# Choosing side tasks by deadline instead of by arrival in a TensorE-bound attention kernel

## The chip, the cores and the metric

The kernel runs on one core of a Trainium2 chip. The core has several engines that work side by side, each through its own list of instructions in order: TensorE (PE, matrix products), VectorE (DVE), ScalarE (ACT, exponentials and copies), GpSimd (POOL, here mostly a second issuer of transfers) and SyncE (SP, which issues most transfers). An engine waits for another by semaphores. The metric is the device time of one execution in microseconds (us): 3230.17 us is the median of three runs of the kernel before (3229.19 to 3231.65).

## The reference

The input `x` is 4 images of 256 channels, 64 x 64 pixels, in float32. Two residual layers follow each other. Both normalize their input in groups of eight channels (`_gn`) and attend with 8 heads of 32 channels.

```python
# layer 0: keys and values come from 2x2 blocks of pixels (1024 keys)
q = jnp.einsum('oc,bchw->bohw', Wq, x)
k = lax.conv_general_dilated(x, Wk, window_strides=(SR, SR), ...)
v = lax.conv_general_dilated(x, Wv, window_strides=(SR, SR), ...)
attn = einsum(q, k) + einsum(q, rel_h + rel_w)
out = einsum(v, softmax(attn * scale))
# layer 1: attention inside four areas of 1024 pixels, a depthwise 7x7 convolution of v, a projection
out = einsum(softmax(q k * scale), v) + _dwconv7(v_full, w_pe, b_pe)
return _conv1x1(out, w_proj, b_proj)
# around them
x = x + layer0(_gn(x)); x = x + layer1(_gn(x))
```

## The kernel before, in words

**Units, steps and phases.** The work is cut into 8 blocks: layer 0 of the four images ("A", b), then layer 1 of the four ("B", b). A block has 16 units; a unit is 512 queries of four heads against 1024 keys. A unit has 8 key steps of 128 keys. The main loop runs in 683 phases, and a phase covers one and a half steps: `scores` (L311) makes the scores of one whole and one half step, ScalarE takes their exponentials (L349, L360), VectorE adds them up for the denominators (L384), and in the next phase `weighted` (L374) multiplies them with the values. A step s falls into phase 2s/3, rounded down. A unit takes 5.33 phases.

**Side work.** Everything else must find room in the phases: normalized inputs, q, k and v, the depthwise convolution, the output projection. `plan_a` and `plan_b` (and `plan_values`, `plan_conv`) write down by `at(unit, step, f)` when a piece is due to be emitted. Loads, normalizations (`normalize`, one ScalarE instruction each, L276), statistics and additions are emitted directly at the end of the phase of their step. Products on TensorE are Python generators put into the list `side` by `task`; each `yield` ends a part. Between the scores and the weighted sums of a phase `side_parts` emits some parts of the first task in the list. All of them share one PSUM bank ("side"), which ScalarE or VectorE empties.

**The order of side work.** `side` is first in, first out. `soon_tasks` puts the q products (L540 and L639) and the projection (L695) at its front. The sum of parts waiting sets the pace: over 4, two parts in a phase; over 8, four; otherwise one. A phase in which a unit's denominators are due (`divisors`, L393) has no other side work. `need` emits side tasks on the spot where the scores ask for a q, k or v that isn't there yet.

**The convolution.** `plan_values` makes the values of an image (`values`, evicted at L833 into one of two `vout` buffers) and stores them to memory in two forms (L838, L846). `load_share` loads, for eight channels, a band matrix (L884) and four sets of rows (L887) from memory. `convolve` (L903) multiplies two such shares, 32 matmuls each, and calls `load_share` for the next ones after each half. There is room for two shares, or three from the second image on. All these transfers are issued by SP in the order of emission, and SP waits where a buffer isn't free.

**The division.** The sum of exponentials of a unit is copied out (L410), spread over partitions by two transfers of GpSimd (L411, L412), inverted on VectorE (`reciprocals`, L418, two units after the unit's start), and broadcast by five transfers (L420, L422) into `rb`. `multiply` (L425) multiplies it on VectorE with the unnormalized output `av_sb`, three units after the unit's start. `av_sb` has two buffers; ScalarE's copy of a unit's output out of PSUM (`evict`, L974) waits for the multiplication of the unit two before.

Of the kernel before, what the change touches and what calls it, by code (L numbers as in the profile page):

```python
# [59 lines left out]
def direct_path(  # L60
# [128 lines left out]
    side, quick = deque(), deque()  # L189
    now, last = [-1], len(BLOCKS) * UNITS * NKT  # L190

    def task(parts, f, *args):
        side.append([parts, f(*args), False])

    def soon_tasks(tasks):

        for n, (parts, f, *args) in enumerate(tasks):
            side.insert((1 if side and side[0][2] else 0) + n, [parts, f(*args), False])

    def advance():  # L200
        side[0][0] -= 1
# [4 lines left out]

    def need(made, key):
        while key not in made:
            advance()
        return made[key]  # L210


    def begun():
        return bool(side) and side[0][2]

    def soon(f):

# [180 lines left out]
    def divide(g, unit):  # L398

        if g == len(units) - 1:  # L400

            rb = pool.tile([P, CH], FP, tag="p", name="rb", bufs=PB)
            V.reciprocal(rb, dens[g])  # L403
            V.tensor_mul(unit[4]()[:, unit[0], :], avs.pop(g), rb)  # L404
            spare.extend((dens.pop(g), rb))
            return
        den_sb = pool.tile([P, CH], FP, tag="cout", name="den_sb", bufs=2)
        few = pool.tile([P, 2, CH // HD], FP, tag="few", name="few", bufs=2)
        rows = dram.tile([4, CH], FP, tag="rows", name=f"rows_{g}", bufs=4)
        S.copy(den_sb, dens.pop(g))  # L410
        G.dma_start(rows, den_sb[0:P:HD, :])  # L411
        G.dma_start(few[:, 0, :], rows.rearrange("h (q n) -> (h q) n", n=CH // HD))  # L412
        made = {}

        def reciprocals():
            rb = made["rb"] = pool.tile([P, CH], FP, tag="rb", name="rb", bufs=1)
            recs = dram.tile([4, CH], FP, tag="recs", name=f"recs_{g}", bufs=4)
            V.reciprocal(few[:, 1, :], few[:, 0, :])  # L418
            V.tensor_reduce(sums[:, :, g], few, AX.X, ALU.add)  # L419
            G.dma_start(recs.rearrange("h (q n) -> (h q) n", n=CH // HD), few[:, 1, :])  # L420
            for h in range(4):
                G.dma_start(rb[HD * h : HD * h + HD, :], recs[h : h + 1, :].to_broadcast([HD, CH]))  # L422

        def multiply():
            V.tensor_mul(unit[4]()[:, unit[0], :], avs.pop(g), made["rb"])  # L425

        at(*((g + 2, 0) if g < len(units) - 2 else (g + 1, 6)), reciprocals)
        at(*((g + 3, 0) if g < len(units) - 3 else (g + 2, 6) if g < len(units) - 2 else (g + 2, 0)), multiply)

    def att_of(key):  # L430
        if key not in atts:
# [4 lines left out]
    def plan_a(b, u, prep):  # L436
# [35 lines left out]
        def make_k(a, qd):  # L472
            if "k" not in taps:
                taps["k"] = k_tile(key)
            k, ps = taps["k"], ps_side(f"k0ps_{b}_{a}_{qd}")[:, :256]
            for n in range(8):
                t, i, w = n // 4, n // 2 % 2, n % 2
                product(
                    ps, lhsT=wk0_sb[:, t, 2 * i + w, qd * P : (qd + 1) * P], rhs=taps[a][:, t, i, w],
                    start=(n == 0), stop=(n == 7),  # L480
                )
                if n % 2 and n < 7:
                    yield
            S.copy(k[:, qd, a * 256 : (a + 1) * 256], ps)
            if a == NAREA - 1:

                rows = k[:, qd, :].rearrange("p (i j) -> p i j", j=32)
                V.tensor_add(rows, rows, relh_sb[:, qd : qd + 1, :].to_broadcast([P, 32, 32]))
                V.tensor_add(rows, rows, relw_sb[:, qd, :].unsqueeze(2).to_broadcast([P, 32, 32]))
                if qd == 1:  # L490
                    ks[key] = k

        def make_v(a, m):
            if "v" not in taps:
                taps["v"] = v_tile(key)
            v, ps = taps["v"], ps_side(f"v0ps_{b}_{a}_{m}")[:, :C]
# [16 lines left out]
        for a in range(NAREA):  # L513
            g = prep + (2 + 3.4 * a if b else 6 + 2.2 * a)
            at(0, int(NKT * (g - 1.6)), lambda a=a: load(a))
            for n in range(8):
                at(0, int(NKT * (g - 1.1)) + n, lambda a=a, n=n: make_taps(a, n))
            for n in range(2):
                at(0, int(NKT * (g + 0.6 * n)), lambda a=a, n=n: task(4, make_k, a, n))
                at(0, int(NKT * (g + 0.6 * n + 1.2)), lambda a=a, n=n: task(4, make_v, a, n))  # L520

        xcs, hqs, made_q = {}, {}, {}

# [4 lines left out]
            normalize(key, hqs[c][:, t, :], hqs[c][:, t, :], t)  # L528

        def make_q(c, qd):  # L530
            if qd == 0:
                made_q[c] = pool.tile([P, 2, CH], FP, tag="q", name=f"q0_{b}_{c}", bufs=2)
            hq, ps = hqs[c], ps_side(f"q0ps_{b}_{c}_{qd}")
# [44 lines left out]
    def plan_b(b, u):  # L578
# [11 lines left out]
        kvs, vcs = {}, {}  # L590

        def make_k(a, qd, half):
            if qd == 0 and half == 0:
                kvs["k"] = k_tile(("B", b, a))
            k, ps = kvs["k"], ps_side(f"k1ps_{b}_{a}_{qd}_{half}")
# [29 lines left out]
                vs["B", b, a] = v  # L625

        def make_q(c, qd):
            if qd == 0:
                kvs["q"] = pool.tile([P, 2, CH], FP, tag="q", name=f"q1_{b}_{c}", bufs=2)
            q, ps = kvs["q"], ps_side(f"q1ps_{b}_{c}_{qd}")  # L630
# [12 lines left out]
        for a in range(NAREA):  # L643
            g = u + 4 * a
            at(g - 6, 3, lambda a=a: load(a))
            for t in range(CT):
                at(g - 5, 2 + 3 * t, lambda a=a, t=t: norm(a, t))
            for n in range(4):
                at(g - 4, 1 + 4 * n, lambda a=a, n=n: task(2, make_k, a, n // 2, n % 2))
            for n in range(4):  # L650
                at(g - 3, 1 + 2 * n, lambda a=a, n=n: load_v(a, n))
                at(g - 2, 1 + 2 * n, lambda a=a, n=n: make_v(a, n))
        for c in range(NCH):
            at(u + 2 * c - 2, 4, lambda c=c: soon_tasks([(2, make_q, c, qd) for qd in range(2)]))

        rest, made_x = {}, {}

# [2 lines left out]
            nc.sync.dma_start(made_x[c], xmid[b][c])  # L660

        def load_rest(c, t):
            if t == 0:
                rest[c] = chunk_tile(f"cv_{b}_{c}")
            cv = rest[c]
# [62 lines left out]
        for c in range(NCH):  # L728
# [75 lines left out]
            for n in range(TX + 6):  # L804
                at(g + 1, 6 * k + n, lambda k=k, n=n: matrices(k, [n]))

    stored = {}

    def plan_values(b, c, start):

# [8 lines left out]

        def values(t):  # L820
            vout = pool.tile([P, RC, TX, XT], FP, tag="vout", name=f"vout_{b}_{c}_{t}", bufs=2)
            V.memset(vout[:, :, :, 0], 0.0)
            V.memset(vout[:, :, :, 1 + WW // TX :], 0.0)
            h = made["h"]
            ps = ps_side(f"vals_ps_{b}_{c}_{t}")
            for tt in range(CT):
# [26 lines left out]
        when = int(start * NKT)  # L853
        at(0, when - 3, load)
        for t in range(CT):
            at(0, when + 5 + t, lambda t=t: norm(t))
# [6 lines left out]
    def load_share(must):  # L863
# [19 lines left out]
        loaded[b, k] = band, xs  # L883
        nc.sync.dma_start(band, mats[k])  # L884
        for a in range(4):
            p = NP // 2 * (a % 2)
# [8 lines left out]
    def convolve(b, n):  # L895
        size = NY * WW // TX
        ps = ps_side(f"conv_ps_{b}_{n}")
        for k in range(2):
            band, xs = loaded.pop((b, 2 * n + k))
            for i in range(2):  # L900
                for half in range(2):
                    for m in range(4):
# [13 lines left out]
            conv[b][16 * n : 16 * n + 16].rearrange("(i c) m y x -> (c m) i (y x)", i=4), out  # L916
        )
        load_share(False)
        yield
# [69 lines left out]

    def side_parts(budget):  # L990

        mine, done = side[0] if side else None, 0
        while done < budget and side and side[0] is mine:
            advance()
            done += 1
# [4 lines left out]

    f = step = 0
    before = []
    while f < PHASES or before or plan or side or quick or to_add or to_divide:
        now[0] = step
        exps = scores(f) if f < PHASES else [lambda: None] * 3
        mine = []
        if f < PHASES:
# [10 lines left out]
        if cut:  # L1018
            evict(before[0][0] // NKT)
        exps[2]()  # L1020
        waiting = sum(n for n, *_ in side)
        if due and not begun():
            g = to_divide.popleft()
            divisors(g, *([last - 1] if g == final else []))
            if g < final:
                divide(g, units[g])
            waiting = 0
        elif cut or waiting > 4 or due or f >= PHASES:
            side_parts(4 if waiting > 8 else 2)
        elif boundary(mine):  # L1030
            side_parts(1 if begun() else 2 if waiting >= 4 else 0)
        else:
# [613 lines left out]
```

## Time and profile before

| | |
|---|---|
| median of three runs | 3230.17 us |
| the profiled execution's own time | 3217.57 us |
| its span, first to last instruction | 3215.8 us |
| TensorE busy | 3088.3 us (96%) |
| VectorE busy | 2525.9 us (79%) |
| ScalarE busy | 2454.4 us (76%) |
| mean granted TensorE clock | 0.985 |

"Busy" is the time in which at least one instruction of the engine ran. The row PE in the page's second part is TensorE's busy share in 40 slices of the span, in tenths; PEclk is the clock that it was granted. In the list of waits a line says which engine and line waited for whom, the total, the number of times and the longest. In a timeline a line has the start, the length, the engine, the line, the operation, what it writes and reads, how many instructions were merged into it, and in brackets the idle time before it and who ended it. PEld are the weight loads of TensorE, which run beside its matmuls.

### The profile page before, as it was taken

How to read it: one execution, taken by the hardware profiler on the slowest of the kernel's cores; microseconds unless marked ns; L12 is line 12 of the kernel's file. 1: busy time of each engine (PE TensorE's matmuls, PEld its weight loads, DVE VectorE, ACT ScalarE, POOL GpSimd, SP SyncE). 2: the span in 40 equal slices, each digit the busy share in tenths (PEclk: the TensorE clock that was granted, in tenths of full speed). 3: DMA queues.
4: the chain of work that ended last, by engine and by line, in shares of the span. 5: the costliest groups of instructions: out<-in, count | busy, mean ns of one | idle time of the engine just before them, and what ended most of it. 6: DMA issues, size and time to landing. Idle time of an engine off the chain costs nothing. (4 is left out here: it accounts for less than half of the span.)

```text
span 3215.8 us, 87826 instructions
## 1 busy us (share of the span) xinstructions
PE 3088.3 (96%) x36218; PEld 1427.4 (44%) x36218; DVE 2525.9 (79%) x2719; ACT 2454.4 (76%) x2988; POOL 486.9 (15%) x923
## 2 busy tenths in 40 slices
PE   7999999999999999998999999999999999999997
PEld 4444444444344554444444444444444444444442
DVE  3687887778776678787677787888878788888887
ACT  3788778887767788887777787787877777787775
POOL 0111121111211111111111111111111111111111
PEclk9999999999999999999999999999999999999999
DMA  5243433555554564567877665655444656633212
GB/s 182 43 105 77 114 90 93 116 119 128 126 136 132 150 166 126 129 151 184 215 192 188 181 164 142 172 154 128 109 97 121 164 159 160 181 102 85 60 43 72
DMA packets 648235, 422.29 MB, mean 131 GB/s; under 512 B 411772, under 2 KB 556636, under 8 KB 647832
## 3 DMA queue, kind: packets, MB, share of 16 engines
q1 hardware_dynamic: 619384, 380.11, 46.8%
q0 software_dynamic: 28448, 36.48, 4.6%
q8 instruction: 293, 4.80, 0.6%
q14 instruction: 110, 0.90, 0.1%
HBM read 318.32 MB, written 98.09 MB: 129 GB/s over the span
## 5 line engine op out<-in xcount | busy, mean ns | idle before, releaser
L384 DVE TENSOR_TENSOR acc<-acc,p 128x1024 f32<-128x1024 f32 x1790 | 2114.9, 1220 | 533.0 <-PE av L374 234.1
L349 ACT ACTIVATE p<-s 128x1024 f32<-128x1024 f32 x1194 | 1160.2, 1027 | 450.7 <-PE s L311 445.4
L360 ACT ACTIVATE p<-s 128x1024 f32<-128x1024 f32 x598 | 620.7, 1038 | 0.4 <-DVE acc L384 0.3
L311 PE MATMUL s<-q,k_A 32*128 32x256 f32 (+1 forms) x5464 | 568.1, 517 | 20.8 <-ACT p L349 10.9
L311 PE MATMUL s<-q,k_B 32*128 32x256 f32 (+1 forms) x5456 | 553.3, 511 | 3.3 <-ACT p L349 3.0
L311 PEld LDWEIGHTS s<-q,k_A 32*128 32x128 f32 x5464 | 342.5, 186 | 309.3 <-ACT p L349 71.2
L311 PEld LDWEIGHTS s<-q,k_B 32*128 32x128 f32 x5456 | 345.4, 184 | 282.8 <-issue 60.8
L374 PE MATMUL av<-p,v_A 128*32 128x256 f32 (+1 forms) x4784 | 457.4, 494 | 0.0
L374 PE MATMUL av<-p,v_B 128*32 128x512 f32 (+1 forms) x4776 | 450.3, 487 | 0.0
L422 POOL DMA_DIRECT2D rb<-recs x508 | 252.0, 501 | 453.6 <-DMA recs<-few 369.2
L374 PEld LDWEIGHTS av<-p,v_B 128*32 128x32 f32 x4776 | 149.5, 110 | 261.6 <-issue 235.9
L420 POOL DMA_DIRECT2D recs<-few x127 | 70.0, 552 | 1229.8 <-DVE sums L419 1193.2
L374 PEld LDWEIGHTS av<-p,v_A 128*32 128x32 f32 x4784 | 150.7, 111 | 236.0 <-issue 198.2
L349 ACT ACTIVATE acc<-s 128x1024 f32<-128x1024 f32 x172 | 167.0, 1024 | 84.8 <-PE s L311 84.7
L903 PE MATMUL conv_ps<-rows,band 88*32 88x128 f32 x3072 | 109.3, 287 | 39.8 <-DMA rows<-vals 39.1
L393 PE MATMUL den<-acc,ones 128*32 128x512 f32 x1024 | 140.2, 607 | 4.8 <-ACT vout L833 3.3
L412 POOL DMA_DIRECT2D few<-rows x127 | 72.3, 569 | 460.9 <-DMA rows<-den_sb 454.7
L411 POOL DMA_DIRECT2D rows<-den_sb x127 | 74.4, 586 | 408.7 <-ACT den_sb L410 402.6
L164 PE MATMUL ops<-cv,wp_sb 128*32 128x512 f32 x1024 | 126.3, 604 | 5.6 <-DVE cv L680 4.4
L164 PE MATMUL q0ps<-hq,wq_sb 128*32 128x512 f32 x1024 | 126.1, 605 | 0.0
L164 PE MATMUL q1ps<-h,wqkv_sb 128*32 128x512 f32 x1024 | 123.3, 598 | 2.2 <-DVE xm L695 2.2
L164 PE MATMUL k0ps<-taps,wkv 128*32 128x256 f32 x2048 | 122.7, 385 | 2.5 <-ACT taps L276 2.5
(99 smaller groups left out, 2200.4 us busy)
## 6 DMA issues: line engine op xcount, KB each, us to landing
rows<-vals SPq DMA_DIRECT2D x384, 195.9 KB
rb<-recs POOLq DMA_DIRECT2D x508, 64.0 KB, 3.1
share<-vals SPq DMA_DIRECT2D x128, 195.9 KB
vala<-vout SPq DMA_DIRECT2D x128, 144.0 KB
vals<-vout SPq DMA_DIRECT2D x128, 144.0 KB
vc<-vala SPq DMA_DIRECT2D x64, 288.0 KB
band<-mats SPq DMA_DIRECT2D x96, 176.0 KB
hq<-in_x SPq DMA_DIRECT2D x32, 512.0 KB
```

The source lines that it names most:

```text
L164: T.matmul(out[cols, :], lhsT=lhsT[:, cols], rhs=rhs, start=start, stop=stop)
L311: return T.matmul(out, lhsT=unit[2]()[rows, unit[0], j * P : (j + 1) * P], rhs=unit[1]()[rows, cols], start=True, stop=True)
L349: S.activation(p, (a, b)[n], AF.Exp, scale=SCALE)
L360: S.activation(p, c.rearrange("p b (l n) -> p b l n", l=2), AF.Exp, scale=SCALE)
L374: T.matmul(out, lhsT=v[:, j, unit[0] * P + HD * h : unit[0] * P + HD * h + HD], rhs=rhs, start=(j == 0 and not u), stop=(j == NKT - 1), sk ...
L384: V.tensor_add(to, to, p)
L393: T.matmul(dens[g][HD * h : HD * h + HD, :], lhsT=ones, rhs=p(h), start=(n == 0), stop=(n == len(sets) - 1),)
L411: G.dma_start(rows, den_sb[0:P:HD, :])
L412: G.dma_start(few[:, 0, :], rows.rearrange("h (q n) -> (h q) n", n=CH // HD))
L420: G.dma_start(recs.rearrange("h (q n) -> (h q) n", n=CH // HD), few[:, 1, :])
L422: G.dma_start(rb[HD * h : HD * h + HD, :], recs[h : h + 1, :].to_broadcast([HD, CH]))
L903: T.matmul(ps[HD * m : HD * m + HD, (2 * k + i) * size : (2 * k + i + 1) * size].rearrange("p (y x) -> p y x", y=NY), lhsT=band[:, half].r ...
```

## The change

Four things change, and some of the planned times with them.

1. Each side task gets a deadline (`due`, in units) and may get a condition (`ready`). `choose` takes, when no task is begun, the able one with the earliest deadline. `soon_tasks` is gone. `pressure` gives the parts waiting and the largest ratio of parts to the phases left until a deadline; two parts are emitted when more than 9 wait or the ratio is above 1, four when it is above 2.
2. A convolution is able only when both of its shares were emitted three phases ago or more; a values task only when the task two before was begun four phases ago or more.
3. Normalizations are put into a queue (`later`); one is emitted at the end of each phase. A task that needs them empties the queue as far as its own go (`settle`).
4. The multiplication by the reciprocals is emitted at (g + 2, 6) for all but the last units, two steps earlier than (g + 3, 0).

```diff
-    def task(parts, f, *args):
-        side.append([parts, f(*args), False])
-
-    def soon_tasks(tasks):
-
-        for n, (parts, f, *args) in enumerate(tasks):
-            side.insert((1 if side and side[0][2] else 0) + n, [parts, f(*args), False])
+    def task(parts, f, *args, due, ready=None):
+
+        side.append([parts, f(*args), False, ready, due * NKT])
+
+    def choose():
+
+        if not begun():
+            able = [n for n, (_, _, _, ready, _) in enumerate(side) if ready is None or ready()]
+            if not able:
+                return False
+            n = min(able, key=lambda n: side[n][4])
+            mine = side[n]
+            del side[n]
+            side.appendleft(mine)
+        return True
+
+    def pressure():
+
+        total, most = 0, 0.0
+        for parts, _, started, ready, due in sorted(side, key=lambda t: t[4]):
+            if started or ready is None or ready():
+                total += parts
+                most = max(most, total / max((due - now[0]) / 1.5 - 1, 1))
+        return total, most
...
+    def later(token, f):
+
+        if now[0] < 0:
+            f()
+        else:
+            norms_left.append((token, f))
+
+    def settle(token):
+
+        while any(t == token for t, _ in norms_left):
+            norms_left.popleft()[1]()
...
-        at(*((g + 3, 0) if g < len(units) - 3 else (g + 2, 6) if g < len(units) - 2 else (g + 2, 0)), multiply)
+        at(g + 2, 6 if g < len(units) - 2 else 0, multiply)
...
+            settle(("taps", b, a))
...
-                at(0, int(NKT * (g - 1.1)) + n, lambda a=a, n=n: make_taps(a, n))
+                at(0, int(NKT * (g - 1.1)) + n, lambda a=a, n=n: later(("taps", b, a), lambda: make_taps(a, n)))
...
-                at(g - 2, 1 + 2 * t, lambda c=c, t=t: norm_chunk(c, t))
-            at(g - 2, 4, lambda c=c: soon_tasks([(2, make_q, c, qd) for qd in range(2)]))
+                at(g - 2, 1 + 2 * t, lambda c=c, t=t: later(("hq", b, c), lambda: norm_chunk(c, t)))
+            for qd in range(2):
+                at(g - 2, 4, lambda c=c, qd=qd, g=g: task(2, make_q, c, qd, due=g - 0.8))
...
-            at(g, j + 2, lambda c=c: soon_tasks([(2, project, c, to) for to in range(CT)]))
+            for to in range(CT):
+                at(g, j + 2, lambda c=c, to=to, g=g: task(2, project, c, to, due=g + 1))
...
-            at(0, when + 7, lambda t=t: task(2, values, t))
+            at(0, when + 7, lambda t=t: task(
+                2, values, t, due=start + 2.5, ready=lambda: written[-2] + 4 <= phase[0]
+            ))
...
-        at(0, when, lambda: task(2, convolve, b, n))
+        def ready():
+            return all(k in loaded and loaded[k][2] + 3 <= phase[0] for k in ((b, 2 * n), (b, 2 * n + 1)))
+
+        at(0, when, lambda: task(2, convolve, b, n, due=start + 1, ready=ready))
...
-            plan_values(b, c, (18.4, 46, 55, 80)[b] + (1.7, 0.8, 1.2, 1.6)[b] * c)
+            plan_values(b, c, (18.4, 46, 54.5, 80)[b] + (1.7, 0.8, 1.2, 1.4)[b] * c)
...
-            plan_conv(b, n, (33, 54.5, 67.5, 96.5)[b] + (0.85, 0.75, 0.95, 0.95)[b] * n)
+            plan_conv(b, n, (33, 54.5, 66.5, 93)[b] + (0.9, 0.85, 0.95, 1.1)[b] * n)
...
-        waiting = sum(n for n, *_ in side)
+        waiting, rate = pressure()
...
-        elif cut or waiting > 4 or due or f >= PHASES:
-            side_parts(4 if waiting > 8 else 2)
+        elif cut or waiting > 9 or rate > 1 or due or f >= PHASES:
+            side_parts(4 if rate > 2 else 2)
...
+        if norms_left:
+            norms_left.popleft()[1]()
```

More of the change, by code (lines that the diff above doesn't have):

```diff
@@ L190, in direct_path @@
     now, last = [-1], len(BLOCKS) * UNITS * NKT
-    def task(parts, f, *args):
-        side.append([parts, f(*args), False])
-    def soon_tasks(tasks):
-        for n, (parts, f, *args) in enumerate(tasks):
-            side.insert((1 if side and side[0][2] else 0) + n, [parts, f(*args), False])
+    phase = [0]
+    def task(parts, f, *args, due, ready=None):
[17 more added lines that the diff above has]
+        return total, most
     def advance():
@@ L208, in need @@
         while key not in made:
+            choose()
             advance()
@@ L214, in begun @@
         return bool(side) and side[0][2]
+    norms_left = deque()
+    def later(token, f):
[6 more added lines that the diff above has]
+            norms_left.popleft()[1]()
     def soon(f):
@@ L495, in make_v @@
                 taps["v"] = v_tile(key)
+            settle(("taps", b, a))
             v, ps = taps["v"], ps_side(f"v0ps_{b}_{a}_{m}")[:, :C]
@@ L516, in plan_a @@
             for n in range(8):
-                at(0, int(NKT * (g - 1.1)) + n, lambda a=a, n=n: make_taps(a, n))
+                at(0, int(NKT * (g - 1.1)) + n, lambda a=a, n=n: later(("taps", b, a), lambda: make_taps(a, n)))
             for n in range(2):
-                at(0, int(NKT * (g + 0.6 * n)), lambda a=a, n=n: task(4, make_k, a, n))
-                at(0, int(NKT * (g + 0.6 * n + 1.2)), lambda a=a, n=n: task(4, make_v, a, n))
+                at(0, int(NKT * (g + 0.6 * n)), lambda a=a, n=n, g=g: task(4, make_k, a, n, due=min(g + 3.5, u)))
+                at(0, int(NKT * (g + 0.6 * n + 1.2)), lambda a=a, n=n, g=g: task(4, make_v, a, n, due=min(g + 4, u)))
         xcs, hqs, made_q = {}, {}, {}
@@ L530, in make_q @@
         def make_q(c, qd):
+            settle(("hq", b, c))
             if qd == 0:
@@ L592, in make_k @@
         def make_k(a, qd, half):
+            settle(("hs", b, a))
             if qd == 0 and half == 0:
@@ L627, in make_q @@
         def make_q(c, qd):
+            settle(("hs", b, c // 2))
             if qd == 0:
@@ L646, in plan_b @@
             for t in range(CT):
-                at(g - 5, 2 + 3 * t, lambda a=a, t=t: norm(a, t))
+                at(g - 5, 2 + 3 * t, lambda a=a, t=t: later(("hs", b, a), lambda: norm(a, t)))
             for n in range(4):
-                at(g - 4, 1 + 4 * n, lambda a=a, n=n: task(2, make_k, a, n // 2, n % 2))
+                at(g - 4, 1 + 4 * n, lambda a=a, n=n, g=g: task(2, make_k, a, n // 2, n % 2, due=g - 1))
             for n in range(4):
@@ L653, in plan_b @@
         for c in range(NCH):
-            at(u + 2 * c - 2, 4, lambda c=c: soon_tasks([(2, make_q, c, qd) for qd in range(2)]))
+            for qd in range(2):
+                at(u + 2 * c - 2, 4, lambda c=c, qd=qd: task(2, make_q, c, qd, due=u + 2 * c - 0.8))
         rest, made_x = {}, {}
@@ L662, in load_rest @@
         def load_rest(c, t):
+            need(convolved, b)
             if t == 0:
@@ L805, in plan_zeros @@
                 at(g + 1, 6 * k + n, lambda k=k, n=n: matrices(k, [n]))
-    stored = {}
+    stored, convolved, written = {}, {}, [-9, -9]
     def plan_values(b, c, start):
@@ L821, in values @@
             vout = pool.tile([P, RC, TX, XT], FP, tag="vout", name=f"vout_{b}_{c}_{t}", bufs=2)
+            written.append(phase[0])
             V.memset(vout[:, :, :, 0], 0.0)
             V.memset(vout[:, :, :, 1 + WW // TX :], 0.0)
+            settle(("hv", b, c))
             h = made["h"]
@@ L855, in plan_values @@
         for t in range(CT):
-            at(0, when + 5 + t, lambda t=t: norm(t))
+            at(0, when + 5 + t, lambda t=t: later(("hv", b, c), lambda: norm(t)))
         for t in range(CT):
-            at(0, when + 7, lambda t=t: task(2, values, t))
+            at(0, when + 7, lambda t=t: task(
+                2, values, t, due=start + 2.5, ready=lambda: written[-2] + 4 <= phase[0]
+            ))
     loaded = {}
@@ L882, in load_share @@
             xs = pool.tile([NP, 2, NY, TC, XT], FP, tag="rows", name=f"rows_{b}_{k}", bufs=2)
-        loaded[b, k] = band, xs
+        loaded[b, k] = band, xs, phase[0]
         nc.sync.dma_start(band, mats[k])
@@ L898, in convolve @@
         for k in range(2):
-            band, xs = loaded.pop((b, 2 * n + k))
+            band, xs, _ = loaded.pop((b, 2 * n + k))
             for i in range(2):
@@ L918, in convolve @@
         load_share(False)
+        if n == C // 16 - 1:
+            convolved[b] = True
         yield
@@ L990, in side_parts @@
     def side_parts(budget):
-        mine, done = side[0] if side else None, 0
+        if not side or not choose():
+            return 0
+        mine, done = side[0], 0
         while done < budget and side and side[0] is mine:
@@ L1002, in direct_path @@
     before = []
-    while f < PHASES or before or plan or side or quick or to_add or to_divide:
-        now[0] = step
+    while f < PHASES or before or plan or side or quick or norms_left or to_add or to_divide:
+        now[0], phase[0] = step, f
         exps = scores(f) if f < PHASES else [lambda: None] * 3
```

## The prediction

> **What bounds the kernel now.** The page first, for the bound and for where it is lost.
>
> ```profile
> span 3215.8 us, 87826 instructions
> ...
> PE 3088.3 (96%) x36218; PEld 1427.4 (44%) x36218; DVE 2525.9 (79%) x2719; ACT 2454.4 (76%) x2988; POOL 486.9 (15%) x923
> ...
> PE   7999999999999999998999999999999999999997
> ...
> PEclk9999999999999999999999999999999999999999
> ```
>
> TensorE is the bound, and nothing in the change takes a matmul away. So only TensorE's waits can be won, and the change can add some. How much work is in a phase (one pass of the main loop, 1.5 key steps) is read from the timeline around 1506 us, undisturbed:
>
> ```profile
> 1505.89 1.59 PE L311 MATMUL s<-q,k_A 32*128 32x256 f32 x16
> ...
> 1507.41 1.92 PE L164 MATMUL vals_ps<-hv,wqkv_sb 128*32 128x512 f32 x16
> ...
> 1508.90 1.03 ACT L360 ACTIVATE p<-s 128x1024 f32<-128x1024 f32 x1
> ...
> 1509.15 1.47 PE L374 MATMUL av<-p,v_A 128*32 128x512 f32 x16
> ...
> 1510.55 1.59 PE L311 MATMUL s<-q,k_A 32*128 32x256 f32 x16
> ```
>
> From one score group to the next it is 4.66 us with a side task of two parts. I measured all 681 intervals this way. The median is 3.80 with one part of q, k, v or a divisor (8 matmuls of 512 columns, 0.86), 4.66 with two, 4.72 with a whole convolution, 6.40 with four. This gives 2.94 + 0.86 per part. With it the loop, from the first score group (81.6 us) to the last (3182.7), needs 2936.8 of its 3101.1 us: 164.3 us are excess. Sorted by what stands in each interval: 65.3 in 15 intervals with convolutions, 13.9 in 11 at half clock after a gap, 23.1 in 30 where ScalarE waits to copy the attention output (av_sb), 25.1 in 35 with no side task, 6.2 at the vout buffers, 4.7 at one late load (xa), the rest 26.0 in small pieces. The waits agree:
>
> ```profile
> PE conv_ps L903 <- DMA rows<-vals: 39.1, 18, 6.6
> ...
> PE av L374 <- ACT av_sb L974: 14.0, 15, 3.1
> PE s L311 <- ACT p L349: 13.9, 30, 1.4
> PE s L311 <- ACT acc L349: 9.7, 7, 4.6
> ...
> PE den L393 <- ACT vout L833: 3.3, 1, 3.3
> ```
>
> Columns: total us, times, longest. Behind the second stands VectorE's multiplication:
>
> ```profile
> ACT av_sb L974 <- DVE att_A L425: 21.6, 13, 3.9
> ...
> ACT av_sb L974 <- DVE att_B L425: 18.7, 16, 2.5
> ```
>
> The worst convolution wait, in the timeline:
>
> ```profile
> 1519.55 2.69 SPq L884 DMA_DIRECT2D band<-mats  x1
> ...
> 1520.82 1.11 PE L903 MATMUL conv_ps<-rows,band 88*32 88x128 f32 x32
> 1522.29 2.31 SPq L887 DMA_DIRECT2D rows<-vals  x4
> ...
> 1528.50 0.66 PE L903 MATMUL conv_ps<-rows,band 88*32 88x128 f32 x8 [6.57 <-DMA rows<-vals]
> ```
>
> The second half started when its rows had not even been issued. And the clock, by stretches (length, five engines, granted clock, DMA share, GB/s), after the gap above and after one of 2.16 us at 433.6:
>
> ```profile
> 437.00:440.40 3.40, 3.16 (x24) 1.64 (x16) 3.05 (x3) 2.61 (x4) 1.98 (x4) 0.50 0.52 111
> 1525.90:1536.10 10.20, 6.42 (x58) 3.73 (x62) 1.06 (x1) 0.59 (x1) 0.57 (x1) 0.50 0.92 243
> ```
>
> A gap just over 2 us costs 3.4 us at half clock, 1.7 us more.
>
> **The change, part by part.** The sum is made against the profiled execution's 3217.57 us; the median of the runs, 3230.17, is 12.6 (0.4%) above it, and I carry the difference over.
>
> *Convolutions wait for loads three phases old.* Of 128 shares, 19 are convolved two phases or less after their loads went out; every stretched one (over 1.2 us for 32 matmuls, usual 1.06 to 1.11) is among them. None of three phases or more is, the tightest at 10.4 us. Three phases are 11.4 to 14 us. At stake: 65.3 plus 6.7 of the half-clock intervals that follow = 72.0. The age counts from the program's emission, and SP can be late: the share above was emitted in phase 309 and issued at 1519.55, some 5 us later; at phase 312 it would still lack about 5 us. Gain 64, ends 55 and 72. The issue per share (a band and four row loads on SP) and the two stores stay with the task; SP already waits 307.3 us at the band load for the convolution before, so nothing queues longer there. A held-back convolution lets another task run.
>
> Band and rows of a share are 176 + 4 x 195.9 = 960 KB, and the one above took 1519.55 to 1530.7, 11 us, from issue to its last matmul. The Trainium skill (DMA: Bandwidth & Descriptors, Anatomy of one DMA) puts a transfer issued from GpSimd at about 2.0 us plus bytes over 436e3. For 960 KB that makes an estimated 4.2 us, by which one phase of age would do and three would hold convolutions back for nothing. The rows above speak against it; by it the sum would keep all 72 of the gain.
>
> *Multiplication two steps earlier (L425).* One VectorE instruction of 0.68 us, no DMA, moves past about four additions: 1.33 phases, 5.7 us. The longest av_sb wait is 3.9, so that wait goes. At stake: 23.1 + 2.3 of half clock = 25.4. In eight divisor intervals (9.7 together) VectorE is simply behind after phases without side work, and the additions would then be late for the divisor: counted as nothing. Gain 16, ends 5 and 25. What it may cost: the multiplication waits on the reciprocals' broadcast (rb), and the additions queue behind it. From last landing to multiplication the slack is 13.1 us in the median, but under 5.7 in five units (5.14, 1.54, 3.15, 5.1, 4.23): VectorE would wait 9.3 us in all. It is 79% busy; I take 2, ends 0 and 9.
>
> *Values wait for their output buffer.* 6.2 us at stake, gain 5, ends 0 and 6. *Late xa load (5.3 us, half clock after):* normalizations now pass a queue, so usually later: gain 2, ends 0 and 6.6. *Intervals without side task:* 25.1 less 6.5 at the start. The new rule takes two parts only above nine waiting or when a deadline presses, so the queue runs dry less often; gain 4, ends -5 (nothing able) and 12.
>
> *One normalization per phase, and the flush.* Some 250 ScalarE instructions (taps 0.65, hq 0.845, hv 0.83 us), no DMA, leave their step. The saving is in the rows above. The new cost is settle(): a task chosen before its normalization has been popped emits it, and all before it, after this phase's exponentials. In the 1506 us timeline the last exponential ends at 1509.93 and the side task would start at 1507.41; a normalization of 0.84 put between ends at 1510.77, so TensorE waits 3.4 us, 0.75 more for each further one, and 1.7 for the clock. In before no such wait shows, since they went out a phase earlier. How often? Step s falls in phase 2s/3. At step 196 the fourth taps set of eight (from 189), two of hq and two of hv arrive within five phases: hq's second is tenth in line, and at the end of phase 130 five have gone; the q task, due in phase 134, finds one to five left. Counted so for all 32 pairs of q tasks in layer 0: certain at steps 196 and 228, likely at 68 and 324 (up to two), possible with one at 100, 148, 356, 388, 420, and three values tasks beside taps. Loss: 2 x 5.9 + 2 x 0.6 x 5.4 + 8 x 0.4 x 5.1 = 34. Ends: 7 (the certain two, one each, no clock) and 67 (all, at their longest). I take 34, since the deadline rule picks q nearly at once.
>
> Of the clock a rule speaks too. The Trainium skill (TensorE: Matmul & The Clock Gate, What's actually happening) has the array throttled after an idle window of about 3.4 us. By it most flushes would cost no clock, an estimated 34 - 6.4 x 1.7 = 23; the 2.16 us gap with its 0.50 row says otherwise here.
>
> *Deadline order.* q and the projections lose their place at the front; a q not made when its unit starts is forced before the scores. With 0.7 unit (3.7 phases) for two tasks of two parts the pressure is above 1 at once. Take 5, ends 0 and 25. Chunk tiles are held about a phase longer; six buffers cover it.
>
> Sum: gains 64 + 16 + 5 + 2 + 4 = 91; losses 2 + 34 + 5 = 41; net 50: 3167.6 against 3217.6, so 3180 for 3230.
>
> **The rivals.** (1) Flushes are common, not rare: then the gains of 84 (91 - 7) are used up at 84/5.5 = 15 flushes. Half of the 64 q and values pairs caught once would be 32 x 5.1 = 163: 3309. For it: the queue's rate of one against 1.5 arrivals per phase in a taps set; against: q's usual two come alone. (2) Convolution loads stay late because SP is late (DMA share 0.92 in the stretch above): half of 64 is lost, 3212. Against: the 10.4 us row. (3) The order moves work about and no wait goes: 3230; only if flushes and gains cancel. (4) Flushes hardly occur, a running task or divisor holding q back for two phases: 34 becomes 8, 3154.
>
> **How the numbers follow.** Forecast 0.47, (1) 0.13, (2) 0.12, (3) 0.05, (4) 0.23. All best ends together give 121.6 - 7 = 115 (3115), all worst ends 55 - 101 = -46 (3276). Leaving out (1) and the far ends of (4) and of the forecast, the range is 3125 to 3232. Faster by over 0.2% (6.5 us, what a measurement of this kernel can tell): 0.47 + 0.12 + 0.23 = 0.82; within 0.05; slower 0.13.
>
> **What would show it.** TensorE's wait for rows under 10 us; ScalarE's av_sb wait on VectorE near 0, at most some us of VectorE waiting on rb; vout waits gone; new waits of TensorE at q0ps or vals_ps on ScalarE's hq or hv, 3.4 us and more, between 0 and 15 of them. It is wrong if these are many, or if scores wait on q or k.

## The result, and the profile after

The changed kernel takes 3220.35 us in the median, the kernel before 3226.03 us when measured beside it: a ratio of 0.9977, with a 95% interval of 0.9965 to 0.9989. So it is faster by about 7 us (0.23%), where 50 were forecast. Single runs of either kernel differ by up to 15 us from their median; the profiled execution of after happens to be a long one (3224.6 us, span 3222.8) and that of before a short one (span 3215.8). So the two profiles are compared by their waits, not by their spans.

The page of after, the same lines as before: span, busy times, TensorE's row in 40 slices, granted clock.

```profile
span 3222.8 us, 87920 instructions
...
PE 3088.0 (96%) x36218; PEld 1423.7 (44%) x36218; DVE 2521.6 (78%) x2719; ACT 2459.6 (76%) x2988; POOL 488.0 (15%) x923
...
PE   7999998999999999989899999999999999999997
...
PEclk9999999999999999999999999999999999999999
```

TensorE is still the bound, and as busy as before. What it waits for has changed. Its waits after (total us, times, longest):

```profile
PE s L345 <- ACT p L383: 23.6, 25, 5.8
PE q0ps L164 <- ACT hq L310: 22.6, 8, 4.7
PE av L408 <- ACT av_sb L1026: 20.0, 19, 1.7
...
PE conv_ps L950 <- DMA share<-vals: 14.9, 6, 4.5
...
PE conv_ps L950 <- DMA rows<-vals: 0.5, 1, 0.5
```

The 39.1 us at the convolution's rows are gone, but 14.9 stand at its shares, where before had:

```profile
PE conv_ps L903 <- DMA share<-vals: 3.1, 3, 1.5
```

The wait of q0ps for hq is new. The wait for the copy of the attention output (av_sb) has grown from 14.0 to 20.0, although VectorE's multiplication no longer holds that copy up (40.3 us before, nothing after).

ScalarE's waits for loads have grown as well; of before one line, of after two:

```profile
ACT taps L276 <- DMA xa<-in_x: 5.3, 1, 5.3
...
ACT taps L310 <- DMA xa<-in_x: 15.3, 3, 7.2
...
ACT hq L310 <- DMA hq<-in_x: 8.7, 3, 6.1
```

I sorted the excess over 2.94 + 0.86 us per part by what stands in each interval between two score groups, as in the prediction (number of intervals in brackets):

| us of excess | before | after |
|---|---|---|
| convolutions | 65.3 (15) | 30.1 (7) |
| av_sb copy waits for VectorE | 23.1 (30) | 0 |
| divisor late, other reasons | 1.6 (3) | 9.6 (10) |
| q waits for a normalization just emitted | 0 | 35.0 (8) |
| no side task | 25.1 (35) | 47.5 (62) |
| ScalarE waits for a load (xa, hq) | 4.7 (2) | 11.6 (5) |
| vout buffers | 6.2 (3) | 5.9 (1) |
| half clock after a gap | 13.9 (11) | 12.9 (8) |
| the rest | 24.5 | 14.2 |
| sum | 164.3 | 166.9 |

The loops themselves, from the first score group to the last, take 3101.1 and 3106.6 us, 5.5 apart, so some 3 us of the excess of after are not in the table. About 58 us were won at the convolutions and the multiplication, and lost again, mostly in the first two of the following places. The third keeps a part of the convolutions' gain back.

**The flush.** The timeline of after around step 196 (start, length, engine, line, what is written and read):

```profile
660.70 1.59 PE L345 MATMUL s<-q,k_A 32*128 32x256 f32 x16
...
662.22 1.06 PE L164 MATMUL q0ps<-hq,wq_sb 128*32 128x512 f32 x8
...
663.81 1.06 ACT L394 ACTIVATE p<-s 128x1024 f32<-128x1024 f32 x1
...
664.71 0.66 ACT L310 ACTIVATE taps<-xa,norm_A 128x256 f32<-128x256 f32 x1
665.22 0.85 ACT L310 ACTIVATE hv<-hv,norm_B 128x512 f32<-128x512 f32 x1
665.93 0.65 ACT L310 ACTIVATE taps<-xa,norm_A 128x256 f32<-128x256 f32 x1
666.44 0.83 ACT L310 ACTIVATE hv<-hv,norm_B 128x512 f32<-128x512 f32 x1
667.15 0.83 ACT L310 ACTIVATE hq<-hq,norm_A 128x512 f32<-128x512 f32 x1
...
668.03 1.81 PE L164 MATMUL q0ps<-hq,wq_sb 128*32 128x512 f32 x8 [4.74 <-ACT hq L310]
```

The q task still needs one normalization, the last of five in the queue; `settle` emits all five behind the phase's last exponential, and TensorE stands for 4.74 us.

**The empty phase at a unit's end.** A phase in which a unit ends and no side task is left:

```profile
1980.93 1.59 PE L345 MATMUL s<-q,k_B 32*128 32x256 f32 x16
...
1982.45 0.64 PE L408 MATMUL av<-p,v_B 128*32 128x256 f32 x8
...
1983.95 0.59 ACT L1026 COPY av_sb<-av 128x512 f32<-128x512 f32 x1
...
1984.59 1.07 PE L408 MATMUL av<-acc,v_B 128*32 128x512 f32 x8 [1.50 <-ACT av_sb L1026]
```

The next unit's weighted sum needs the one PSUM bank that ScalarE empties behind its exponentials. A side task would lie in between; without one TensorE waits 1.50 us. Of the 19 waits at av_sb 16 stand in intervals without a side task, with 17.9 of the 20.0 us.

**A share that SP issues late.** The timeline of SP, and the convolution that waits:

```profile
1713.41 5.10 SPq L891 DMA_DIRECT2D vals<-vout  x2
...
1716.86 1.11 PE L950 MATMUL conv_ps<-share 88*32 88x128 f32 x32
...
1718.63 3.20 SPq L883 DMA_DIRECT2D vala<-vout  x2
...
1721.88 2.20 SPq L891 DMA_DIRECT2D vals<-vout  x2
...
1726.58 0.32 SPq L931 DMA_DIRECT2D share<-mats  x1
...
1735.67 0.66 PE L950 MATMUL conv_ps<-share 88*32 88x128 f32 x8 [4.51 <-DMA share<-vals]
...
1738.56 1.52 PE L950 MATMUL conv_ps<-share 88*32 88x128 f32 x24 [2.22 <-DMA share<-vals]
```

The share's load was written into the program right after the convolution at 1716.86, so it was old enough by the program's phases; SP came to it about 9 us later, behind stores that took it 2 to 5 us each.

### The profile page after: what moved, and what is told of

Read it like the earlier page. It is cut to its first block, busy times and chain, and to the rows that moved or that the text cites. A ratio compares the mean times of both kernels' runs of the same rounds, so it can differ in the third digit from the quotient of the medians.

```text
span 3222.8 us, 87920 instructions
## 1 busy us (share of the span) xinstructions
PE 3088.0 (96%) x36218; PEld 1423.7 (44%) x36218; DVE 2521.6 (78%) x2719; ACT 2459.6 (76%) x2988; POOL 488.0 (15%) x923
## 4 chain that ended last, share of the span: by engine, by line
PE 67%; DMA 7%; ACT 3%; DVE 3%; issue 2%; SPq 1%; ACTq 0%; DVEq 0%; POOL 0%; POOLq 0%
PE s L345 23%; PE av L408 19%; PE k1ps L164 3%; PE ops L164 3%; PE q1ps L164 3%; PE conv_ps L950 3%; PE vals_ps L164 3%; PE den L427 3%; PE q0ps L164 2%; DVE acc L418 2%; DMA rows<-vals 2%; PE v0ps L164 2%; ACT p L383 2%; PE k0ps L164 1%; DMA share<-vals 1%
## 5 line engine op out<-in xcount | busy, mean ns | idle before, releaser
L345 PE MATMUL s<-q,k_B 32*128 32x512 f32 (+1 forms) x5456 | 553.2, 510 | 2.9 <-ACT p L383 2.3
L383 ACT ACTIVATE acc<-s 128x1024 f32<-128x1024 f32 x172 | 166.9, 1023 | 90.1 <-PE s L345 89.9
L164 PE MATMUL vals_ps<-hv,wqkv_sb 128*32 128x512 f32 x1024 | 123.3, 597 | 1.2 <-ACT vout L878 0.9
L164 PE MATMUL k1ps<-h,wqkv_sb 128*32 128x512 f32 x1024 | 124.3, 598 | 0.0
```

The lines of the kernel that those rows point to most:

```text
L164: T.matmul(out[cols, :], lhsT=lhsT[:, cols], rhs=rhs, start=start, stop=stop)
L345: return T.matmul(out, lhsT=unit[2]()[rows, unit[0], j * P : (j + 1) * P], rhs=unit[1]()[rows, cols], start=True, stop=True)
L383: S.activation(p, (a, b)[n], AF.Exp, scale=SCALE)
```

## The experiments

All ratios are to the kernel before, measured beside each run. Differences between two runs are worked out from their ratios, with 3226 us for 1.

**The flush and the pace.** Theory 1 was that the flushes took the gain, theory 2 that they only take the blame, theory 3 that the pressure of deadlines runs the list of side tasks dry. In the first run a q task is held back until its normalizations are out:

```diff
+    def emitted(token):
+        return all(t != token for t, _ in norms_left)
...
-                at(g - 2, 4, lambda c=c, qd=qd, g=g: task(2, make_q, c, qd, due=g - 0.8))
+                at(g - 2, 4, lambda c=c, qd=qd, g=g: task(
+                    2, make_q, c, qd, due=g - 0.8, ready=lambda: emitted(("hq", b, c))))
```

> The changed kernel, but a q task of layer 0 is able only once its two normalizations have left the queue, so that none is flushed. Theory 1 (the flushes are where the gain went): the profile after has 8 intervals in which TensorE waits for hq at q0ps, with 35.0 us of excess and some 3 us of half clock behind them. Without them the time falls by 25 to 38 us against the changed kernel, to 0.986 to 0.990 of the kernel before, and the wait of q0ps on hq is gone. Theory 2 (the flush only takes the blame: TensorE would have waited for ScalarE in the next phases anyway): less than 10 us, 0.995 or more. Theory 3 (the pace, not the flush, ate the gain): also less than 10 us.

Measured: 3193.62 us, 0.9893 (0.9876 to 0.9911), 27 us less than the changed kernel. The longest waits of TensorE in that run, one in the start left out:

```profile
PE av L411 <- ACT av_sb L1030: 20.9, 20, 2.0
PE s L348 <- ACT p L386: 18.0, 27, 5.4
...
PE conv_ps L954 <- DMA share<-vals: 10.3, 6, 3.0
```

q0ps no longer waits for hq (one values task still waits 2.7 us for its hv), and the wait at av_sb stays. Theory 1 holds with its number; theory 2 falls, and so does theory 3 as the only cause.

The next run leaves out the queue altogether:

```diff
     def later(token, f):
-        if now[0] < 0:
-            f()
-        else:
-            norms_left.append((token, f))
+        f()
```

> The changed kernel without the queue of normalizations: each is emitted at the end of its own step's phase again, the rest as changed. Theory 1 (flushes): as the run in which q waits, 0.986 to 0.990 of before, if the queue itself smooths nothing. If one normalization per phase is worth something by itself, this run is slower than that one by 5 to 15 us. Theory 2: within 10 us of the changed kernel.

Measured: 3198.07 us, 0.9907 (0.9889 to 0.9924). The flush is gone here too. The difference to the run with the queue, 0.0014 or 5 us, is within the intervals: what one normalization per phase is worth by itself stays open between nothing and some 12 us.

Then the old pace:

```diff
-        elif cut or waiting > 9 or rate > 1 or due or f >= PHASES:
-            side_parts(4 if rate > 2 else 2)
+        elif cut or waiting > 4 or due or f >= PHASES:
+            side_parts(4 if waiting > 8 else 2)
```

> The changed kernel with the old pace (more than 4 parts waiting: two, more than 8: four) in place of the pressure of deadlines; choice by deadline, ages and the queue stay. Theory 3 (the pressure runs the queue dry): phases without side work fall from 67 to 40 by the order of emission; at 0.8 us of excess each (47.5 us in 62 intervals) the time falls by 15 to 25 us against the changed kernel, to 0.990 to 0.993 of before. Theory 1 alone: no change, 0.9977, since 7 flushes of q remain.

Measured: 3181.65 us, 0.986 (0.984 to 0.9881), 38 us less than the changed kernel and more than theory 3 had expected. Its waits show both why and where the surplus is from:

```profile
PE q0ps L164 <- ACT hq L310: 12.2, 4, 4.1
...
PE av L408 <- ACT av_sb L1026: 9.4, 10, 1.1
```

The wait at av_sb is halved, as the empty phases fall (47.5 us in 62 intervals to 27.1 in 42). But the flushes are fewer too, four of q and one of values in place of eight of q: 35.0 us of excess become 21.5. That q is taken less quickly at the old pace is the likely reason; it was not shown. The two causes overlap. The version with both mended separates them:

```diff
-        elif cut or waiting > 9 or rate > 1 or due or f >= PHASES:
-            side_parts(4 if rate > 2 else 2)
+        elif cut or waiting > 4 or due or f >= PHASES:
+            side_parts(4 if waiting > 8 else 2)
...
+                    2, make_q, c, qd, due=g - 0.8, ready=lambda: emitted(("hq", b, c))))
...
-                2, values, t, due=start + 2.5, ready=lambda: written[-2] + 4 <= phase[0]
+                2, values, t, due=start + 2.5, ready=lambda: written[-2] + 4 <= phase[0] and emitted(("hv", b, c))
```

> The changed kernel with the old pace, and with q and values tasks able only once their normalizations have left the queue. If the two losses add up (27 us by q alone, 38 us by the pace alone, and 21.5 us of flushes left with the old pace), it comes to 3155 to 3168 us, 0.978 to 0.982 of before. If a q task held back is forced later by the scores and costs as much, it stays at 0.985 or more.

Measured: 3174.62 us, 0.9824 (0.9811 to 0.9837), less than the sum. The four make a square:

| ratio to before | new pace | old pace |
|---|---|---|
| flushes | 0.9977 | 0.986 |
| q held back (at the old pace the values too) | 0.9893 | 0.9824 |

The pace is worth 22 us without flushes (0.9893 to 0.9824) and 38 with them; the flushes 27 us at the new pace and 12 at the old. The traces of the lower row agree with the 22: all intervals without a side task, 68 with 50.5 us of excess, become 46 with 27.5.

Why the pressure empties the list can be counted in the order of emission, as the program writes it. Of the 544 phases in which no divisor is due, the ratio of parts to phases left is above 2 in 237 and above 1 in 165 more; over nine parts wait in only 5 beyond these. In 54 of the 544 the list is empty, and in 13 it has tasks but none that is able. The deadlines of q, the projection and the convolution stand 3 to 6 phases from their start (q 0.7 unit, a convolution one), and the count keeps one phase spare, so these tasks press almost from the first. That the old pace mends this is shown; that looser deadlines would was not run.

**The age of the loads.** First taken out of the changed kernel:

```diff
-            return all(k in loaded and loaded[k][2] + 3 <= phase[0] for k in ((b, 2 * n), (b, 2 * n + 1)))
+            return all(k in loaded for k in ((b, 2 * n), (b, 2 * n + 1)))
```

> The changed kernel without the age of the loads: a convolution is able as soon as its two shares have been emitted. If the age is what removed the waits for rows (39.1 us before, 0.5 after, but shares 3.1 to 14.9), these come back and the time rises by 25 to 60 us against the changed kernel, to 1.006 to 1.016 of before. If the choice by deadline alone spaces the convolutions, it stays within 10 us of the changed kernel.

Measured: 3267.05 us, 1.0124 (1.0103 to 1.0146), 47 us more than the changed kernel. The waits are back, at the rows and the shares:

```profile
PE conv_ps L950 <- DMA share<-vals: 24.5, 8, 12.1
...
PE conv_ps L950 <- DMA rows<-vals: 19.1, 14, 2.9
```

The choice by deadline does not space the convolutions by itself; the age does. Then the age alone, put into the kernel before:

```diff
+    def choose():
+        if not begun():
+            n = next((n for n, t in enumerate(side) if t[3] is None or t[3]()), None)
+            if n is None:
+                return False
+            mine = side[n]
+            del side[n]
+            side.appendleft(mine)
+        return True
...
-        at(0, when, lambda: task(2, convolve, b, n))
+        def ready():
+            return all(k in loaded and loaded[k][2] + 3 <= phase[0] for k in ((b, 2 * n), (b, 2 * n + 1)))
+
+        at(0, when, lambda: task(2, convolve, b, n, ready=ready))
```

> The kernel before with the age of the loads alone: still first in, first out, but a convolution whose shares are less than three phases old is passed over. By the prediction's largest term it gains 55 to 72 us: 0.978 to 0.983 of before, with no wait for rows over 2 us. If late issue on SP keeps a part of the waits, as it did for the shares in the changed kernel (14.9 us, three of 2.4 to 4.5 us), it gains 30 to 45: 0.986 to 0.991.

Measured: 3197.57 us, 0.9893 (0.9877 to 0.9909), 35 us. The second expectation holds: a part of the waits stays, 8.7 and 5.9 us:

```profile
PE conv_ps L916 <- DMA rows<-vals: 8.7, 7, 2.3
PE conv_ps L916 <- DMA share<-vals: 5.9, 3, 3.9
```

And a part is given back: with convolutions held there are 48 intervals without side work in place of 35, with 37.8 us of excess in place of 25.1.

One phase more of age, in the combined version:

```diff
-            return all(k in loaded and loaded[k][2] + 3 <= phase[0] for k in ((b, 2 * n), (b, 2 * n + 1)))
+            return all(k in loaded and loaded[k][2] + 4 <= phase[0] for k in ((b, 2 * n), (b, 2 * n + 1)))
```

> The combined version (old pace, q and values held until their normalizations are out) with an age of four phases in place of three. In the combined version two convolutions still wait for shares that SP issued late (6.9 and 6.4 us of excess with their half clock). If a phase more covers SP's delay, these go and the time falls by 8 to 14 us against the combined version, to 0.978 to 0.980 of before. If holding convolutions back empties phases or forces q, nothing is won: 0.982 or more.

Measured: 3152.17 us, 0.9781 (0.9756 to 0.9805), 14 us less than with three phases. The excess at convolutions falls from 19.0 to 3.1 us. So a fixed age by the program's phases had to cover SP's delay here as well as the transfer.

**The multiplication.** Back at its old step in the changed kernel, and alone in the kernel before:

```diff
-        at(g + 2, 6 if g < len(units) - 2 else 0, multiply)
+        at(*((g + 3, 0) if g < len(units) - 3 else (g + 2, 6) if g < len(units) - 2 else (g + 2, 0)), multiply)
```

> The changed kernel with the multiplication by the reciprocals back at its old step. If the earlier multiplication gains what the prediction gave it (16 us, ends 5 and 25), this run is slower than the changed kernel by as much, 1.000 to 1.005 of before, and ScalarE waits for the multiplication at av_sb again (40 us before, 0 after). If what is won there is lost again where the additions are late for the divisor, it stays within 5 us of the changed kernel, 0.996 to 0.999.

> The kernel before with the earlier multiplication alone. By the prediction it gains 14 us (5 to 25): 0.992 to 0.998 of before, with ScalarE's wait for it at av_sb near 0. If the wait only moves, 0.998 to 1.001.

Measured: 0.9989 (0.9978 to 1.0001) with the old step in the changed kernel, which gives the new step 4 us, not clear of nothing; and 0.9955 (0.9942 to 0.9967) with the new step alone, 14.5 us. In both kernels the copy no longer waits for VectorE. In the run of the multiplication alone what is left at av_sb is the wait for TensorE itself:

```profile
ACT av_sb L974 <- PE av L374: 18.5, 26, 5.2
```

In the changed kernel the excess at av_sb falls from 20.1 us to none by the earlier step, but the excess at divisors that wait for VectorE's last additions is 9.6 in place of 4.1 us. TensorE's own waits for them, 5.1 and 4.2 us, differ less, so that a part of the wait moves there is likely and not shown.

The age and the multiplication alone, 35 and 14.5 us in the kernel before, would make 49 if they add up, and the combined version, the whole change without its pace and its flushes, has 57. So the choice by deadline, the queue, the values' condition and the new planned times may be worth little beyond the other two. Of these only the queue was taken out by itself, so this is not shown.

**A version that beats both.** Two more losses were left in the combined version: ScalarE waits for a late load of the taps' input (xa, 13.6 us in three waits), and the first load of the second image's convolution forces values out in one go. The latter in the changed kernel, in the timeline:

```profile
1411.06 4.27 SPq L891 DMA_DIRECT2D vals<-vout  x2
...
1414.46 0.70 ACT L878 ACTIVATE vout<-vals_ps,bqkv_sb 128x512 f32<-128x512 f32 x1 [8.20 <-DMA vals<-vout]
```

The forced third value waits for its buffer, and ScalarE with it, 8.20 us. The two runs:

```diff
-            at(0, int(NKT * (g - 1.6)), lambda a=a: load(a))
+            at(0, int(NKT * (g - 2.4)), lambda a=a: load(a))
```

> The combined version with the loads of the taps' input (xa) planned 0.8 unit earlier. ScalarE waits there twice for about 6 us in the combined version (9.9 us of excess, 4.4 more in the intervals behind). If SP's lateness is the cause and there are chunk buffers free, this falls by 8 to 14 us, to 0.978 to 0.980 of before. If the buffers are full, SP waits for one and other loads come late: no gain, 0.981 or more.

Measured: 3149.67 us, 0.977 (0.9748 to 0.9792), 17 us less than the combined version. The excess at loads falls from 9.9 to 2.4 us, that at half clock from 18.0 to 3.4, and, by luck or not, that at convolutions from 19.0 to 11.9. Then both, with four phases of age:

```diff
-            plan_conv(b, n, (33, 54.5, 66.5, 93)[b] + (0.9, 0.85, 0.95, 1.1)[b] * n)
+            plan_conv(b, n, (33, 55.5, 66.5, 93)[b] + (0.9, 0.85, 0.95, 1.1)[b] * n)
```

> Both together, and the second image's convolutions planned one unit later (55.5), so that fewer values are forced out at its first load (two chunks in the combined version, 8.9 us of excess). If all three add up, 3145 to 3160 us, 0.974 to 0.979 of before; if the first two are worth nothing, 3165 to 3175.

Measured: 3140.33 us, 0.9747 (0.9725 to 0.9768): 82 us less than the kernel before, and 25 less than the combined version. That is less than the 31 us of its first two parts one by one, so they overlap; the convolutions' later start was not run alone. Its page:

```profile
span 3138.3 us, 87933 instructions
...
PE 3057.5 (97%) x36218; PEld 1416.9 (45%) x36218; DVE 2519.6 (80%) x2719; ACT 2455.8 (78%) x2988; POOL 486.1 (15%) x923
...
PE   7999999999999999999999999999999999999997
...
PEclk9999999999999999999999999999999999999999
```

The dips of TensorE's row are gone but for start and end, and the mean granted clock is 0.997 in place of 0.985. From the first score group to the last it takes 3023.1 us, 78.0 less than before with the same work, so about 86 of the 164.3 us of excess remain. 47 intervals have no side task.

## Why the prediction was wrong

The reading of the bound held: TensorE, no matmul taken away, some 164 us of waits. The time lies inside the stated range, and the sign is as forecast, but the sign is partly luck: what was won and what was lost nearly cancel. Rival 3 (3230) comes nearest in number. Its condition, that flushes and gains cancel, nearly came true, with the pace beside the flushes, but not that "no wait goes": about 58 us went. The runs give 47 (age) + 4 (multiplication) - 27 (flush) - 22 (pace) = 2 us against the 7 measured; the prediction's sum was 50. (The flush and the pace are taken out here one after the other, together 49 us; runs that take one thing out of a whole need not add up.) By its terms:

- *Convolutions, 64 (55 to 72)*: right mechanism, too large. It measured 35 us alone and 47 in the changed kernel. I had kept 8 us for SP's delay, from the one case that the trace of before showed. (By the order of emission that share went out in phase 310 and not 309, and 17 shares and not 19 were convolved two phases or less after; neither changes the term.) After, SP's delay sat at the shares, in three convolutions with 3.5 to 6.7 us of TensorE's waits each, and phases left empty by held convolutions were not counted. Rival 2 (half lost to SP's lateness, 3212) had this mechanism.
- *Multiplication, 16 less 2 (5 to 25)*: 14.5 us alone, as forecast. In the changed kernel 4 us, with an interval that reaches to nothing; there a part of the wait may have moved to the divisor; where the rest went stays open. VectorE's wait for rb, put at 9.3 us in all, was 2.4 there and 8.9 in the kernel before with the multiplication alone.
- *Values and vout, 5*: nothing. One wait remained, longer than those before, because the values are forced at the first load of the convolutions; the condition does not hold for a forced task. That term I had put under deadline order (5 us): the intervals around 1400 to 1420 us show 9.8.
- *Late xa load, gain 2*: wrong in sign. The excess at late loads, xa and hq together, went from 4.7 us to 11.6, and planning the xa loads earlier won 17 us from the combined version. What made them later in the changed kernel was not settled.
- *Flushes, 34 (7 to 67; its terms add up to 34.6)*: right in kind and place. Some six were expected and eight found, at the q tasks of steps 68, 100, 196, 228, 324, 356, 388 and 420, with 35.0 us of excess; the listed step 148 and the values had none. That the sum fits so closely is partly luck, more flushes at 4.4 us each in place of fewer at 5.1 to 5.9, and holding q back won 27 us and not all 35. Rival 4, that they hardly occur, falls; so does rival 1, since the 15 that it needs were not reached.
- *Intervals without side task, gain 4 (-5 to 12)*: this is the step that failed. "So the queue runs dry less often" was read off the thresholds and not off the deadlines: with 0.7 unit for two tasks I noted myself that the pressure is above 1 at once, and did not draw the consequence for the other tasks. In place of a gain of 4 us, 25.1 us of excess became 47.5, and the pace costs 22 us once the flushes are gone.

With the pace at -22 in place of +4 and the age at 47 in place of 64 the prediction's sum comes to 7. The other deviations (multiplication 10 less, flush 7 less, loads and values) are smaller and of both signs; how they share the rest was not settled.

Of the clock: of the eight flushes, with gaps of 2.0 to 4.7 us, seven were followed by half clock for 3.4 us, as the row of 2.16 us in the prediction suggested; one of 2.7 us was not. Six of the gaps were of 2.8 us or less, and five of these were followed by half clock. The shortest, and the one that was not, in the timeline:

```profile
1282.02 1.40 PE L164 MATMUL q0ps<-hq,wq_sb 128*32 128x512 f32 x8 [2.02 <-ACT hq L310]
...
1082.39 1.06 PE L164 MATMUL q0ps<-hq,wq_sb 128*32 128x512 f32 x8 [2.72 <-ACT hq L310]
```

And the stretches after the first and around the second:

```profile
1282.60:1286.00 3.40, 3.40 (x28) 0.74 (x16) 3.37 (x4) 0.59 (x1) 0.18 (x1) 0.50 0.32 128
1079.00:1087.00 8.00, 5.28 (x56) 1.99 (x52) 5.48 (x8) 5.59 (x9) 0.55 (x1) 1.00 0.85 221
```

The granted clock, third from the end, is 0.50 and 1.00.

## What to carry to other kernels

A pace that is set by deadlines can press nearly all the time, as it did here: count, in the order of emission, how often it is pressed and how often the list runs empty before trusting it. When work is put into a queue that a consumer may flush, give the consumer a condition instead, since a flush puts the work behind the busiest part of the phase. An age counted in the program's phases must also cover the delay of the queue that issues the load.

## What was not expected of the hardware

SP's issue of one and the same transfer takes very different times. In the changed kernel the store of the values took SP 0.382 us at least, 0.940 in the median and 5.149 at most:

```profile
L891 SPq DMA_DIRECT2D vals<-vout x128: 382/940/5149, 536.3 to 2375.5; - x128
```

The loads on SP queue behind it in order: the share of the timeline above was issued about 9 us late, with its buffer free since the convolution at 1716.86, and its last matmuls waited until 1738.56, 12 us after its issue began. The Trainium skill (DMA: Bandwidth & Descriptors, Anatomy of one DMA), weighed in the prediction, would have had an estimated 4.2 us for a share's band and rows, by a fit for transfers issued from GpSimd. The 12 us, and the 14 us that four phases of age won over three, are against planning by that figure for SP's loads here.
